# A four-layer graph network on one core: PSUM operands in layer 3, edges loaded first, layer 0's sums turned by transposes, node stages in halves

## The chip, the core and the metric

The kernel runs on one NeuronCore of a Trainium2 chip. The metric is the device time of one execution in microseconds (us), lower is better. The core has five engines that run at the same time, each with its own list of instructions: TensorE (PE, with its weight loads shown apart as PEld), VectorE (DVE), ScalarE (ACT), GpSimd (POOL) and SyncE (SP). DMA transfers are issued from the queues of SP, ACT and POOL. SBUF is the memory that all engines work on; PSUM is the one PE writes its products to, in banks of 512 float32 per partition.

## The reference

The input is a graph of 12,500 nodes with 32 features and 212,500 edges, sorted by destination (200,000 drawn ones and a loop for every node). Four layers follow one another, each as `x = layernorm(x + layer(x))`:

```python
# layer 0: weighted gather, segment sum, matmul
z = segment_sum(x[src] * edge_weight[:, None], dst) @ W
# layer 1: an MLP on edges with two batch norms, summed by source node
ef = concat([x[src], x[dst]])
h = relu(batch_norm(ef @ W1 + b1)); h = relu(batch_norm(h @ W2 + b2))
out = segment_sum(h, src)
# layer 2: two graph convolutions, norm = rsqrt(deg)[src] * rsqrt(deg)[dst]
h = h @ W; agg = segment_sum(h[src] * norm, dst) + h / deg + b
# layer 3: a 32x32 matrix per edge, six steps of a GRU
w_e = (relu(e_feat @ en1.T + b) @ en2.T + b).reshape(-1, 32, 32)
for _ in range(6):
    msg = einsum('ei,eio->eo', h[src], w_e)
    h = gru_cell(relu(segment_sum(msg, dst) + conv_bias), h)
```

## The kernel before

**Tiling.** Edges are padded to 128 x J with J = 1664 tile columns; a column is 128 edges, a chunk is CB = 32 columns, and NCH = 52 chunks are one pass over the edges. Nodes lie in SBUF as 128 partitions x NH = 98 columns x 32 features. A flag `crowded` (L658), worked out from the edges, selects between this path and a slower one that isn't executed here.

**Gathers and scatters.** A column of 128 rows is fetched by one indirect DMA that POOL issues (`gather`, L325, all recorded as L326). Scatters of 128 rows stand at L1686 (records of edges, by source, `rec_t`) and L1152 (`own_t`). A pass over the edges is 1664 of these on POOL.

**Stages in order.**
1. *Head*: SP loads the weights, then `by_tiles` (L582) loads dst, src and edge weights in rows of tiles, turns them with PE transposes (L606) and copies them out of PSUM on DVE (L607). The survey counts edges per node by one-hots on DVE (L377) and matmuls (L385). `places` (L396) makes the starts of nodes from the counts and tests that no tile of 128 edges begins too many nodes: it builds one-hots of each node's start (`oh_tile`, `oh_high`, L456), multiplies them on PE in 98 matmuls (L464) and takes the maximum (L466). The flag ends the head. Then the scatters by source node run.
2. *Layer 0's segment sum*: `slot_sum` (L984) reads the records chunk by chunk (`load`, L1721). A comparison of each edge's slot with an iota makes a mask; PE multiplies it with the edges' values into `acc` (L917); DVE keeps the block of its own (`part`, L927) and runs a scan over the columns (`running`, L934, with the comparison `on` at L938, the carry copy at L949, the scan at L952); ACT reorders (`by8`, L964); PE sums quarters back with `stack` (L1004, `back`), ACT copies to `o` and SP stores a table. At its end 98 gathers fetch the nodes' sums (`agg`).
3. *Node stage of layer 0*: transposes of `agg`, product with W, layernorm over all 98 columns, transposes of x, product with layer 1's weights, two tables written.
4. *Layer 1*: first pass with 26 gathers of runs (`run_rows`) and 1664 of `gq`, second pass without gathers, `slot_sum` again, 98 gathers, layernorm.
5. *Layer 2*: `kept` and `both` are made from x over all columns (L1145 to L1150), 98 scatters, and two convolutions of 1664 gathers each. Their comparisons use `iota_q`, a copy of iota in PSUM, and their `part` is in PSUM.
6. *Layer 3* (`layer3_tiles`, L1284): six steps. For each chunk DVE makes `near` (L1299, a comparison from SBUF into PSUM), ACT copies it to `mask`; 32 columns are gathered from the states in two halves; for each pair of columns DVE makes `prod` (L1322), PE multiplies with the edge's hidden values into `m` (L1330), ACT writes `outer` (L1337). Then PE makes `sums` (L917) and `acc` (L1354, L1362). The remaining work of a chunk (scan, by8, GRU gates, new state; L1367 to L1428) is spread over the pairs of the next chunk by the table `later`. Buffers: `g` 4, `eh` 3, `prod` and `m` 2, `near`, `sums`, `acc` and `gates` 1 (a PSUM bank each; `m` two banks a buffer).
7. *End*: a last layernorm per slot and 98 gathers of nodes.

**What sets the order.** The kernel is written in a tile framework: its scheduler places instructions on each engine's list, and dependencies between tiles follow from the regions that are read and written. A pool gives a tile so many buffers; a new tile of the same tag waits until the oldest buffer has been read.

Of the kernel before, what the change touches and what calls it, by code (L numbers as in the profile page):

```python
# [45 lines left out]
P = 128  # L46
# [28 lines left out]
MAGIC = 12582912.0  # L75

# [7 lines left out]
def tile_gnn(ctx: ExitStack, tc: tile.TileContext, a: dict, out: bass.AP):  # L84
# [6 lines left out]
    def sb(pool, shape, dt, name, **kw):  # L91
        return pool.tile(shape, dt, name=name, tag=name, **kw)

# [187 lines left out]
    def transposed(psum, xt, x):  # L281

        for g0 in range(0, CG, 4):
            n = min(4, CG - g0)
            t = sb(psum, [P, 4, P], F32, "tp")
            for k in range(n):
                g = g0 + k
                nc.tensor.transpose(t[:, k, :], x[:, 4 * g : 4 * g + 4, :].rearrange("p c f -> p (c f)"), ident)
            nc.vector.tensor_copy(xt[:, g0 : g0 + n, :], t[:, 0:n, :])

    def linear(psum, xt, w, width, use):

        for g in range(CG):
            t = sb(psum, [P, 4, width], F32, f"lin{width}")
            nc.tensor.matmul(
                t.rearrange("p c f -> p (c f)"), xt[:, g, :], w.rearrange("p c f -> p (c f)"), start=True, stop=True
            )
            use(g, t)
# [4 lines left out]
    def layernorm(name, x, d, y):  # L303

        with tc.tile_pool(name=f"ln_{name}", bufs=1) as work:
            s = sb(work, [P, NH, F], F32, "s")
            q = sb(work, [P, NH, F], F32, "q")
            m = sb(work, [P, NH], F32, "m")
            v = sb(work, [P, NH], F32, "v")
            nc.vector.tensor_add(s, x[:, 0:NH, :], d[:, 0:NH, :])  # L310
            nc.vector.tensor_reduce(out=m, in_=s, axis=AX, op=ALU.add)
            nc.vector.tensor_scalar(m, m, 1.0 / F, None, op0=ALU.mult)
            nc.vector.tensor_tensor(s, s, m.unsqueeze(2).to_broadcast([P, NH, F]), op=ALU.subtract)
# [4 lines left out]
            nc.vector.tensor_tensor(y[:, 0:NH, :], s, v.unsqueeze(2).to_broadcast([P, NH, F]), op=ALU.mult)  # L318

    def node_array(pool, name):  # L320
        t = sb(pool, [P, C, F], F32, name)
        nc.vector.memset(t[:, NH:C, :], 0.0)
        return t

# [23 lines left out]
    slots_ = ctx.enter_context(tc.tile_pool(name="slots", bufs=1))  # L348
# [47 lines left out]
    def places(work, psum, k, count, bad=None):  # L396
# [41 lines left out]
        if bad is not None:  # L438
# [5 lines left out]

            nc.vector.tensor_copy(at[:, 0, :], start[k])
            nc.vector.tensor_scalar(at[:, 1, :], at[:, 0, :], 7, None, op0=ALU.arith_shift_right)
            nc.vector.tensor_scalar(at[:, 2, :], at[:, 0, :], 14, None, op0=ALU.arith_shift_right)
            nc.vector.tensor_scalar(at[:, 1, :], at[:, 1, :], 127, None, op0=ALU.bitwise_and)
            nc.vector.tensor_copy(atf, at)
            nc.vector.scalar_tensor_tensor(atf[:, 2, :], atf[:, 2, :], 1.0, some, op0=ALU.add, op1=ALU.mult)  # L450
            nc.vector.tensor_scalar(atf[:, 2, :], atf[:, 2, :], -1.0, None, op0=ALU.add)
            tiles = J // P
            x = sb(work, [P, NH, P], BF, "oh_tile", bufs=1)
            y = sb(work, [P, NH, tiles], BF, "oh_high", bufs=1)
            for t, w_, d in ((x, P, atf[:, 1, :]), (y, tiles, atf[:, 2, :])):
                nc.vector.tensor_tensor(  # L456
                    t,
                    iota[:, 0:w_].unsqueeze(1).to_broadcast([P, NH, w_]),
                    d.unsqueeze(2).to_broadcast([P, NH, w_]),
                    op=ALU.is_equal,  # L460
                )
            starts = sb(psum, [P, tiles], F32, "starts")
            for h_ in range(NH):
                nc.tensor.matmul(starts, x[:, h_, :], y[:, h_, :], start=h_ == 0, stop=h_ == NH - 1)  # L464
            most = sb(work, [P, 1], F32, "most")
            nc.vector.tensor_reduce(out=most, in_=starts, axis=AX, op=ALU.max)  # L466
            nc.vector.tensor_scalar(most, most, WS - 0.5, None, op0=ALU.is_gt)
# [114 lines left out]
    def by_tiles(work, psum, name, to, firsts=None):  # L582

        v = a[name].rearrange("(b t p) -> t b p", p=P, t=P)
        whole = v.dtype == I32
        t = sb(work, [P, J // P, P], v.dtype, "by_i" if whole else "by_f")
        nc.sync.dma_start(t, v)
        if whole:
            f = sb(work, [P, J // P, P], F32, "by_f")
            nc.vector.tensor_copy(f, t)  # L590
            if name == "src":
# [5 lines left out]
                nc.sync.dma_start(saved["lo_row"].rearrange("o (b t p) -> t (o b) p", p=P, t=P), b)  # L597
# [4 lines left out]
        for b0 in range(0, J // P, 4):  # L602
# [4 lines left out]
            nc.vector.tensor_copy(to[:, b0 * P : (b0 + n) * P], u[:, 0:n, :].rearrange("p b t -> p (b t)"))  # L607
# [57 lines left out]
    fast_.close()  # L665

# [317 lines left out]
    def slot_sum(name, table, fill, agg, k="d", first=None):  # L984


        W, R8, slot_, going_, iota_w_ = (
            (W_D, R8_D, slot, going, iota_w) if k == "d" else (WS, P, slot_s, going_s, iota_s)
        )
        with tc.tile_pool(name=f"sl_{name}", bufs=2) as work, tc.tile_pool(  # L990
# [3 lines left out]
            for c in range(NCH):  # L994
# [7 lines left out]
                back = sb(psum, [R8, KB, F], F32, "back", bufs=1)  # L1002
                for b in range(KB):
                    nc.tensor.matmul(back[:, b, :], by8[:, b, :], stack, start=True, stop=True)  # L1004
                o = sb(work, [R8, KB, F], F32, "o")
                nc.scalar.activation(o, back, AF.Copy)
                nc.sync.dma_start(by_chunk(table, c, R8), o)
        for c in range(NH):
            gather(agg[:, c, :], table, slot_end[k][:, c : c + 1])
# [127 lines left out]
    def layer2_tiles(x):  # L1137

        spread = []
        with tc.tile_pool(name="n2", bufs=1) as n2:  # L1140
# [4 lines left out]
            nc.vector.tensor_tensor(both[:, :, 0:F], x[:, 0:NH, :], wide, op=ALU.mult)  # L1145
            nc.vector.tensor_copy(both[:, :, F], slot_end["d"])
            write_table("t2s", both, F + 1)
            kept = sb(n2, [P, NH, F + 1], F32, "kept")
            nc.scalar.activation(kept[:, :, 0:F], x[:, 0:NH, :], AF.Copy)
            nc.vector.tensor_copy(kept[:, :, F], root)  # L1150
            for c in range(NH):
# [54 lines left out]
        def fetch_a(work, c):  # L1206
            t = sb(work, [P, CB, F + 1], F32, "g33", bufs=3)
            for j in range(CB):
                gather(t[:, j, :], tables["t2s"], idx_d[:, c * CB + j : c * CB + j + 1])
# [31 lines left out]
        def fetch_b(work, c):  # L1241
            g = sb(work, [P, CB, F], F32, "g", bufs=3)
            for j in range(CB):
                gather(g[:, j, :], sums[0], idx_t[:, c * CB + j : c * CB + j + 1])
# [39 lines left out]
    def layer3_tiles():  # L1284

        def step(k, old_, new, mhs):
            with tc.tile_pool(name=f"l3{k}", bufs=2) as work, tc.tile_pool(
# [4 lines left out]

                def at(p):
# [3 lines left out]
                for c in range(NCH):  # L1297
                    near = sb(psum, [P, CB, W], F32, "near")
# [3 lines left out]
                        iota_w.unsqueeze(1).to_broadcast([P, CB, W]),  # L1302
# [8 lines left out]
                    for b in range(2):  # L1311
                        t0 = c * CB + b * HB
                        g = sb(work, [P, HB, F], F32, "g", bufs=4)
                        for j in range(HB):
                            gather(g[:, j, :], old_, idx_t[:, t0 + j : t0 + j + 1])
# [28 lines left out]
                    sums_ = sb(psum, [P, CB, W], F32, "sums")  # L1344
# [22 lines left out]
                    def run_on(c=c, acc=acc, v={}):  # L1367
# [6 lines left out]
                            iota_w,  # L1374
                            lambda out: nc.scalar.activation(out, acc.rearrange("p (t w) -> p w t", w=W), AF.Copy),  # L1375
                        )
# [36 lines left out]
                    def first_two(st=st):  # L1413
                        rz = st["rz"] = sb(work, [R8, KB, 2, F], F32, "rz")
                        nc.scalar.activation(rz, st["gates"][:, :, 0:2, :], AF.Sigmoid)
                        n = st["n"] = sb(work, [R8, KB, F], F32, "n")
# [3 lines left out]
                    def third(st=st):  # L1420
                        nc.scalar.activation(st["n"], st["n"], AF.Tanh)

                    def stored(st=st, old=old, c=c):
                        d = sb(work, [R8, KB, F], F32, "d")
                        nc.vector.tensor_sub(d, old, st["n"])
                        nc.vector.tensor_mul(d, d, st["rz"][:, :, 1, :])
                        nc.vector.tensor_add(d, st["n"], d)
# [131 lines left out]
    def by_source_tiles():  # L1559
# [143 lines left out]
        slot_all = sb(src, [P, J + 1], F32, "slot_s")  # L1703
# [5 lines left out]
        with tc.tile_pool(name="n0t", bufs=1) as n0:  # L1709
            ends = [sb(n0, [P, P], F32, f"row{p}") for p in (0, P - 1)]  # L1710
# [8 lines left out]
            with tc.tile_pool(name="l0t", bufs=3) as rec, tc.tile_pool(name="l0p", bufs=2, space=PSUM) as pp:  # L1719

                def load(c):  # L1721
# [8 lines left out]
                    nc.vector.tensor_copy(idx_s[:, js], t[:, :, F])  # L1730
# [8 lines left out]
                    nc.vector.tensor_copy(es, e)  # L1739
# [15 lines left out]
                slot_sum("l0", sums_s[0], fill, agg, "s", lambda c: loaded.update({c: load(c)}))  # L1755
            aggt = sb(n0, [P, CG, P], F32, "aggt")
            z = sb(n0, [P, C, F], F32, "z")
            with tc.tile_pool(name="p0t", bufs=2, space=PSUM) as psum:
                transposed(psum, aggt, agg)
                linear(psum, aggt, w0, F, lambda g, t: nc.vector.tensor_copy(z[:, 4 * g : 4 * g + 4, :], t))  # L1760
            layernorm("0t", x, z, x)

        with tc.tile_pool(name="n1t", bufs=1) as n1:
            pt, qt = sb(n1, [P, C, F], F32, "pt"), sb(n1, [P, C, F], F32, "qt")
            xt = sb(n1, [P, CG, P], F32, "xt")
            with tc.tile_pool(name="p1t", bufs=2, space=PSUM) as psum:
                transposed(psum, xt, x)

                def use(g, t):
                    nc.scalar.activation(pt[:, 4 * g : 4 * g + 4, :], t[:, :, 0:F], AF.Copy)  # L1770
                    nc.vector.tensor_tensor(qt[:, 4 * g : 4 * g + 4, :], t[:, :, F:], bias(b1_row, 4), op=ALU.add)

                linear(psum, xt, w1, 2 * F, use)
            write_table("t1q", qt)
            nc.sync.dma_start(tables["t1p"].rearrange("(c p) f -> p c f", p=P)[:, 0:NH, :], pt[:, 0:NH, :])
# [44 lines left out]
        with ExitStack() as l1:  # L1820
# [4 lines left out]
            with tc.tile_pool(name="p1at", bufs=2, space=PSUM) as psum, tc.tile_pool(  # L1825
# [10 lines left out]
                def fetch(c):  # L1836
                    gq = gqs[c] = sb(wide, [P, CB, F], F32, "gq", bufs=3)
                    for j in range(CB):
                        gather(gq[:, j, :], tables["t1q"], idx_s[:, c * CB + j : c * CB + j + 1])
# [83 lines left out]
            with tc.tile_pool(name="p1dt", bufs=2, space=PSUM) as pd:  # L1923
# [16 lines left out]
                slot_sum("l1", sums_s[1], fill, agg, "s")  # L1940
# [223 lines left out]
```

## Time and profile before

| | us |
|---|---|
| median of 3 runs (lowest to highest) | 23281.31 (23269.91 to 23287.24) |
| profiled execution | 23284.4 |
| its span in the profile | 23282.1 |
| granted TensorE clock, mean | 0.791 |
| busy: PE / DVE / ACT / POOL | 15635.5 / 10162.4 / 7142.4 / 16401.7 |

The profile is of one execution. It gives busy time by engine, the span in 40 slices, the chain of work that ended last, and groups of instructions: line, engine, operation, `out<-in`, shapes, count, then busy us and mean ns of one, then the idle time ahead of them and what ended it. Further views of the trace list an engine's waits (`line <- releaser: us in total, times, longest us`), a timeline of single instructions (start us, us, engine, line, operation, idle time ahead), and busy time by engine in chosen stretches of the span. Line numbers are those of the code above. POOL's part in a gather or scatter is the issue of it; the transfer follows on DMA engines.

### The profile page before, as it was taken

The page shows a single profiled execution, that of the slowest core. Times are in us where ns is not written, and L with a number is a line of the kernel's source. Part 1 is how long each engine was busy: PE and PEld are TensorE (multiplying, and loading weights), DVE is VectorE, ACT ScalarE, POOL GpSimd, SP SyncE. Part 2 cuts the span into 40 slices and gives each one's busy share as a digit, 9 for nine tenths or more (in the row PEclk, how much of TensorE's full clock was granted, in tenths as well). Part 3 has the DMA queues.
Part 4 walks back from the last instruction along what each step waited for, and adds up shares of the span by engine and source line. Part 5 has one row for each costly group of instructions (what it writes and reads, how often), then busy time and mean ns, then how long its engine had stood idle before and what let it go on. Part 6 is the DMA issues. An engine that isn't in the chain of part 4 may idle for free. (4 is left out here: it accounts for less than half of the span.)

```text
span 23282.1 us, 220871 instructions
## 1 busy us (share of the span) xinstructions
PE 15635.5 (67%) x73549; PEld 8950.4 (38%) x73549; DVE 10162.4 (44%) x16060; ACT 7142.4 (31%) x11020; POOL 16401.7 (70%) x17092
## 2 busy tenths in 40 slices
PE   4777644447122211148888888888888888888885
PEld 3666633335011111124444444444444444444442
DVE  7666434446111111124544444444444444544443
ACT  0333211114000000024444444444444444444442
POOL 2777357772777777777777777777777777777776
PEclk7555557778555555569999999999999999999997
DMA  2111223333111111112222222222222222222222
GB/s 66 43 42 41 58 78 94 94 94 116 17 17 16 16 19 19 19 42 69 67 69 65 68 69 64 68 67 69 64 69 69 67 64 69 67 66 67 68 69 57
DMA packets 1162538, 1372.56 MB, mean 59 GB/s; under 512 B 632424, under 2 KB 1024104, under 8 KB 1061320
## 3 DMA queue, kind: packets, MB, share of 16 engines
q1 hardware_dynamic: 597256, 952.79, 12.9%
q0 software_dynamic: 549184, 296.38, 8.2%
q10 hardware_dynamic: 14976, 109.06, 1.1%
q8 instruction: 627, 10.27, 0.2%
q14 instruction: 495, 4.06, 0.1%
HBM read 1130.72 MB, written 226.28 MB: 58 GB/s over the span
## 5 line engine op out<-in xcount | busy, mean ns | idle before, releaser
L326 POOL DMA_INDIRECT g<-states,idx_t x9984 | 9628.0, 964 | 3208.7 <-issue 2828.0
L1330 PE MATMUL m<-prod,eh 128*128 128x416 f32 x19968 | 8081.6, 548 | 1430.3 <-DVE prod L1322 1308.9
L1322 DVE TENSOR_TENSOR prod<-g,near 128x832 f32<-128x832 f32 x4992 | 5040.8, 1020 | 5142.6 <-DMA g<-states,idx_t 3243.4
L1330 PEld LDWEIGHTS m<-prod,eh 128*128 128x128 f32 x19968 | 3723.2, 199 | 5461.2 <-issue 4142.8
L1337 ACT ACTIVATE outer<-m 128x832 f32<-128x832 f32 x4992 | 4477.1, 897 | 4368.5 <-PE m L1330 4360.8
L917 PE MATMUL acc<-mask,g 128*128 128x52 f32 x1664 | 456.2, 420 | 3407.6 <-ACT g L1212 1725.8
L1686 POOL DMA_INDIRECT rec_t<-record,to x1664 | 1601.5, 962 | 675.0 <-issue 501.4
L326 POOL DMA_INDIRECT g<-sums,idx_t x1664 | 1571.6, 944 | 526.7 <-issue 492.2
L326 POOL DMA_INDIRECT gq<-t1q,idx_s x1664 | 1585.1, 953 | 507.1 <-issue 487.3
L326 POOL DMA_INDIRECT g<-t2s,idx_d x1664 | 1570.2, 944 | 515.2 <-issue 494.9
L1354 PE MATMUL acc<-outer,en_i 128*32 128x416 f32 x19968 | 1812.8, 515 | 0.0
L917 PEld LDWEIGHTS acc<-mask,g 128*128 128x128 f32 x1664 | 389.7, 321 | 3482.0 <-issue 1737.8
L1354 PEld LDWEIGHTS acc<-outer,en_i 128*32 128x32 f32 x19968 | 617.6, 110 | 979.7 <-issue 961.8
L1663 PE MATMUL place<-cur,xt 128*128 128x98 f32 x3326 | 990.7, 426 | 0.8 <-DVE own L1668 0.2
L952 DVE TENSOR_TENSOR_SCAN s<-on,part 128x429 f32<-128x429 f32 (+1 forms) x520 | 574.7, 1105 | 779.6 <-ACT part L1375 772.4
L964 ACT ACTIVATE by<-s 128x416 f32<-128x416 f32 (+1 forms) x520 | 293.9, 565 | 2013.8 <-DVE s L952 2013.8
L1663 PEld LDWEIGHTS place<-cur,xt 128*128 128x128 f32 x3326 | 814.9, 302 | 226.3 <-DVE own L1668 126.8
L927 DVE TENSOR_TENSOR part<-acc,blk 128x512 f32<-128x512 f32 (+1 forms) x208 | 134.3, 646 | 1663.0 <-PE acc L917 1663.0
L1375 ACT ACTIVATE part<-acc 128x416 f32<-128x416 f32 x312 | 162.1, 520 | 2261.8 <-PE acc L1362 2261.8
L1877 PE MATMUL t<-ident,gq 128*128 128x128 f32 x832 | 239.1, 383 | 899.6 <-DMA gq<-t1q,idx_s 830.7
L1662 ACT ACTIVATE cur<-next 128x98 f32<-128x98 f32 x1663 | 421.3, 253 | 1347.7 <-PE place L1663 790.0
L326 POOL DMA_INDIRECT agg<-sums_s,slot_end_s x196 | 185.0, 944 | 913.1 <-issue 912.2
(384 smaller groups left out, 16628.4 us busy)
## 6 DMA issues: line engine op xcount, KB each, us to landing
eh<-edge_h SPq DMA_DIRECT2D x624, 1024.0 KB
g<-states,idx_t POOLq DMA_INDIRECT x9984
edge_h<-eh ACTq DMA_DIRECT2D x104, 1024.0 KB
lows<-lo_row SPq DMA_DIRECT2D x52, 1024.0 KB
ht<-h_t SPq DMA_DIRECT2D x104, 512.0 KB
rt<-rec_t SPq DMA_DIRECT2D x52, 544.0 KB
rec_t<-record,to POOLq DMA_INDIRECT x1664
attr<-in_edge_attr SPq DMA_DIRECT2D x52, 512.0 KB
```

What stands on the lines that cost most here:

```text
L326: nc.gpsimd.indirect_dma_start(out=to, out_offset=None, in_=table, in_offset=bass.IndirectOffsetOnAxis(ap=idx, axis=0))
L917: nc.tensor.matmul(acc[:, 4 * g : 4 * g + 4, :].rearrange("p t w -> p (t w)"), v, mask[:, 4 * g : 4 * g + 4, :].rearrange("p t w -> p (t w)"),
L952: nc.vector.tensor_tensor_scan(s.rearrange("p w t -> p (w t)"), on.rearrange("p w t -> p (w t)"), part_.rearrange("p w t -> p (w t)"), ini ...
L964: nc.scalar.activation(by8.rearrange("p b (w t) -> p w b t", t=8), s[:, :, 1:].rearrange("p w (b t) -> p w b t", t=8), AF.Copy)
L1322: nc.vector.tensor_tensor(prod, g[:, j : j + 2, :].unsqueeze(3).to_broadcast([P, 2, F, W]), near[:, jj : jj + 2, :].unsqueeze(2).to_broadc ...
L1330: nc.tensor.matmul(m[:, i, 0 : F * W], eh[:, j + i, :], prod[:, i].rearrange("p f w -> p (f w)"), start=True, stop=True,)
L1337: nc.scalar.activation(outer[:, :, jj : jj + 2, :].rearrange("k f t w -> k t f w"), m[:, :, 0 : F * W].rearrange("k t (f w) -> k t f w", w=W),
L1354: nc.tensor.matmul(acc[q * F : (q + 1) * F, :], en2_i[:, i, :], outer[:, i].rearrange("k t w -> k (t w)"), start=i < 4, stop=i >= F - 3, s ...
L1662: nc.scalar.activation(cur, nxt, AF.Copy)
L1663: nc.tensor.matmul(place[:, j, :], xt[:, j, :], now, start=True, stop=False)
L1686: i = nc.gpsimd.indirect_dma_start(out=rec_t, out_offset=bass.IndirectOffsetOnAxis(ap=to[:, j : j + 1], axis=0), in_=t[:, j, :], in_offset ...
L1877: nc.tensor.matmul(t[:, g, :], gq[:, jj : jj + 4, :].rearrange("p j f -> p (j f)"), ident, start=True, stop=False)
```

## The change

- **Loads.** `src`, `dst` and `edge_weight` are the first loads on SP's queue, into tiles of their own. `by_tiles` uses them, writes `lo_row` from ACT's queue instead of SP's, and copies transposes out of PSUM on ACT instead of DVE.
- **Test of tiles.** In `places` the one-hots and 98 matmuls are replaced by two matmuls that fetch, for each node, the start of the node WS places on, and a comparison of the tile numbers of both.
- **Layer 0's segment sum.** Where `slot_sum` has a `first` (layer 0), `back` is made by four transposes of `by8` and a reduction on DVE. The copies to `idx_s` and `es` are on ACT; slots and the `ends` matrices are bf16 (slots in layer 1's masks too).
- **Halves.** `transposed`, `linear` and `layernorm` take a range of columns; layer 0's node stage and layer 1's layernorm, with the copies `kept` and `both`, are written for columns 0 to 51 and 52 to 97 in turn.
- **Gathers.** `gather_tiles` leaves out the columns beyond the last real edge (TILES = 1661) and sets their rows to zero.
- **Layer 3.** `near` and a copy of iota share one PSUM bank made once a step; `near` and `on` compare with that copy. `part` lies in the bank of `sums`. `n` after tanh, and the difference `old - n`, are written into the `gates` bank.

```diff
+TILES = -(-E // P)
+    for name in ("src", "dst", "edge_weight"):
+        raw[name] = sb(raw_pool, [P, J // P, P], a[name].dtype, f"raw_{name}")
+        nc.sync.dma_start(raw[name], a[name].rearrange("(b t p) -> t b p", p=P, t=P))
...
+    HALVES = ((0, -(-CG // 2)), (-(-CG // 2), CG))
...
+    def gather_tiles(to, table, idx, t0):
+
+        n = min(to.shape[1], max(0, TILES - t0))
+        if n < to.shape[1]:
+            nc.vector.memset(to[:, n:, :], 0.0)
+        for j in range(n):
+            gather(to[:, j, :], table, idx[:, t0 + j : t0 + j + 1])
...
+            far = sb(work, [P, 2, P], F32, "far")
+            for i in range(2):
+                nc.vector.tensor_scalar(far[:, i], iota, float(WS - 1 - i * P), part[:, 0:1], op0=ALU.add, op1=ALU.is_equal)
+            nc.tensor.matmul(below, far[:, 0], start[k], start=True, stop=False)
+            nc.tensor.matmul(below[:, 0 : NH - 1], far[:, 1], start[k][:, 1:NH], start=False, stop=True)
...
-                nc.sync.dma_start(saved["lo_row"].rearrange("o (b t p) -> t (o b) p", p=P, t=P), b)
+                nc.scalar.dma_start(saved["lo_row"].rearrange("o (b t p) -> t (o b) p", p=P, t=P), b)
...
-            nc.vector.tensor_copy(to[:, b0 * P : (b0 + n) * P], u[:, 0:n, :].rearrange("p b t -> p (b t)"))
+            nc.scalar.activation(to[:, b0 * P : (b0 + n) * P], u[:, 0:n, :].rearrange("p b t -> p (b t)"), AF.Copy)
...
+                if first is not None:
+                    back = sb(psum, [R8, KB, P], F32, "back", bufs=1)
+                    for b in range(KB):
+                        nc.tensor.transpose(back[:, b, :], by8[:, b, :], ident)
+                    nc.vector.tensor_reduce(
+                        out=o, in_=back.rearrange("r b (q f) -> r b f q", f=F), axis=AX, op=ALU.add
+                    )
...
+            for half in HALVES:
+                cs = slice(4 * half[0], min(NH, 4 * half[1]))
+                nc.scalar.activation(kept[:, cs, 0:F], x[:, cs, :], AF.Copy)
+                nc.vector.tensor_tensor(both[:, cs, 0:F], x[:, cs, :], wide[:, cs, :], op=ALU.mult)
+                nc.sync.dma_start(tables["t2s"].rearrange("(p c) f -> p c f", p=P)[:, cs, :], both[:, cs, :])
...
+                bank = sb(psum, [P, 512], F32, "near")
+                near = bank[:, 0:CW].rearrange("p (t w) -> p t w", w=W)
+                iota_q = bank[:, CW : CW + W]
+                nc.vector.tensor_copy(iota_q, iota_w)
...
-                        iota_w.unsqueeze(1).to_broadcast([P, CB, W]),
+                        iota_q.unsqueeze(1).to_broadcast([P, CB, W]),
...
-                    sums_ = sb(psum, [P, CB, W], F32, "sums")
+                    sums_ = sb(psum, [P, 512], F32, "sums")[:, 0:CW].rearrange("p (t w) -> p t w", w=W)
...
-                            iota_w,
+                            iota_q,
                             lambda out: nc.scalar.activation(out, acc.rearrange("p (t w) -> p w t", w=W), AF.Copy),
+                            sb(psum, [P, 512], F32, "sums")[:, 0 : W * (CB + 1)].rearrange("p (w t) -> p w t", w=W),
...
-                            nc.scalar.activation(st["n"], st["n"], AF.Tanh)
+                        nc.scalar.activation(st["gates"][:, :, 0, :], st["n"], AF.Tanh)
...
-                        nc.vector.tensor_sub(d, old, st["n"])
-                        nc.vector.tensor_mul(d, d, st["rz"][:, :, 1, :])
-                        nc.vector.tensor_add(d, st["n"], d)
+                        n, e = st["gates"][:, :, 0, :], st["gates"][:, :, 1, :]
+                        nc.vector.tensor_sub(e, old, n)
+                        nc.vector.tensor_mul(d, e, st["rz"][:, :, 1, :])
+                        nc.vector.tensor_add(d, n, d)
...
-        slot_all = sb(src, [P, J + 1], F32, "slot_s")
+        slot_all = sb(src, [P, J + 1], BF, "slot_s")
-            ends = [sb(n0, [P, P], F32, f"row{p}") for p in (0, P - 1)]
+            ends = [sb(n0, [P, P], BF, f"row{p}") for p in (0, P - 1)]
-                    nc.vector.tensor_copy(idx_s[:, js], t[:, :, F])
+                    nc.scalar.activation(idx_s[:, js], t[:, :, F], AF.Copy)
-                    nc.vector.tensor_copy(es, e)
+                    nc.scalar.activation(es, e, AF.Copy)
...
+                for h, half in enumerate(HALVES):
+                    transposed(psum, aggt, agg, half)
+                    linear(
+                        psum, aggt, w0, F, lambda g, t: nc.vector.tensor_copy(z[:, 4 * g : 4 * g + 4, :], t), half
+                    )
+                    layernorm(f"0t{h}", x, z, x, half)
+                    transposed(psum, aggt, x, half)
+                    linear(psum, aggt, w1, 2 * F, use, half)
...
-            layernorm("1t", x, agg, x)
+            for h, half in enumerate(HALVES):
+                layernorm(f"1t{h}", x, agg, x, half)
```

## The prediction

> **What bounds the kernel now.** I began with the page's busy times: POOL 70%, PE 67%, nothing else above 44%. The slices of the span show POOL at 7 tenths nearly everywhere with PE at 8 to 9 in the second half, so both are candidates. The chain that ended last is led by POOL's gathers of 128 rows, and the groups say how these run:
>
> ```profile
> L326 POOL DMA_INDIRECT g<-states,idx_t x9984 | 9628.0, 964 | 3208.7 <-issue 2828.0
> L326 POOL DMA_INDIRECT g<-sums,idx_t x1664 | 1571.6, 944 | 526.7 <-issue 492.2
> L326 POOL DMA_INDIRECT gq<-t1q,idx_s x1664 | 1585.1, 953 | 507.1 <-issue 487.3
> ```
>
> Behind each gather stand about 0.305 us put down to issue, in which POOL waits for nobody. A gather costs 1.249 us in layer 2 (0.944 + 0.305) and 1.269 in layer 3 (0.964 + 0.305). So in the streams of gathers POOL is full, although it reads 70%, and the time is streams plus the gaps between them. The wait list of POOL gives the gaps:
>
> ```profile
> POOL rec_t L1686 <- PE place L1663: 167.8, 1, 167.8
> ...
> POOL agg L326 <- issue: 912.2, 193, 431.2
> ...
> POOL run_rows L326 <- DVE eh L1814: 67.2, 1, 67.2
> ...
> POOL own_t L1152 <- ACT kept L1149: 28.1, 1, 28.1
> ```
>
> Reading along the span: POOL starts its stream of scatters at 477.6 us; 1664 scatters run to 2586; 431.2 us go to layer 0's segment sum; 98 gathers; 67.2; layer 1's gathers to 5334; a second pass of 423 us; 98 gathers, 28.1, 98 scatters; two streams of layer 2 (6039 to 10214); six streams of layer 3 (10231 to 23051) with gaps of 26 to 35 us; 232 us of end. The six streams are 12,820 of 23,282 us. There the work by engine is:
>
> ```profile
> 10231.00:23050.00 12819.00, 11281.29 (x51060) 5560.58 (x51060) 6302.42 (x8103) 5472.72 (x7174) 9627.19 (x9984) 0.96 0.24 67
> ```
>
> Columns are PE, PEld, DVE, ACT, POOL. Over 312 chunks (6 steps of 52) PE is busy 36.2 us a chunk, and POOL needs 32 x 1.269 = 40.6 us. **PE has 4.4 us to spare in a chunk**, and POOL sets the pace.
>
> **Layer 3's operands in PSUM.** Why are its gathers 20 ns longer than layer 2's? Most are not: they take 0.94, and two in every chunk are long. The timeline of POOL around one chunk:
>
> ```profile
> 16224.94 1.21 POOL L326 DMA_INDIRECT g<-states,idx_t  x1 [0.30 <-issue]
> 16226.45 0.94 POOL L326 DMA_INDIRECT g<-states,idx_t  x1 [0.30 <-issue]
> ...
> 16236.44 1.37 POOL L326 DMA_INDIRECT g<-states,idx_t  x1 [0.30 <-issue]
> 16238.12 0.94 POOL L326 DMA_INDIRECT g<-states,idx_t  x1 [0.30 <-issue]
> ```
>
> and DVE's of the same moments:
>
> ```profile
> 16224.74 0.60 DVE L1299 TENSOR_TENSOR near<-slot,iota_w 128x416 f32<-128x416 bf16 x1
> ...
> 16236.31 0.18 DVE L949 COPY part<-s 128x13 f32<-128x13 f32 x1
> 16236.40 0.60 DVE L938 TENSOR_TENSOR on<-going,iota_w 128x429 f32<-128x429 bf16 x1
> ```
>
> Over 14,600 to 16,600 us the long gathers fall together with these operations: all 49 near cost 253 ns beyond 944, all 49 on (with the copy ahead of it) 427 ns; together 34 us in 1576 gathers. The operations at L1425 and L1426, also of two SBUF tiles, cost gathers nothing. In layer 2 the same two comparisons take iota from PSUM and the copy goes into PSUM:
>
> ```profile
> L938 DVE TENSOR_TENSOR on<-going,iota_q 128x429 f32<-128x429 bf16 x49 | 29.0, 593 | 0.0
> L976 DVE TENSOR_TENSOR mask<-slot,iota_q 128x416 f32<-128x416 bf16 x48 | 27.9, 581 | 0.0
> ```
>
> and there gathers average 944. The change makes layer 3 like layer 2. It takes away (253 + 427) ns x 312 chunks = **212 us**, bounds 0 (the cause is something else in layer 3) and 225 (34.25 us of excess in 1576 gathers is 0.0217 us, x 9984 = 217, and some at the edges). I take 212. DVE's own time does not grow: near and on take 600 ns from SBUF in layer 3, 593 and 581 with PSUM in layer 2; the scan 1079 and 1049.
>
> [...]
>
> The new cost: part now lies in the bank of sums (one buffer), and near and iota_q fill one bank for the whole step (one buffer, as before). PE's sums of a chunk must wait until the scan of the chunk before has read part. In the changed program's order the scan stands in the first quarter of a chunk on DVE and most of sums at the end on PE, so there are about 20 us between them. Cost 0; above, PE's whole reserve, 4.4 less the 0.7 that POOL gains = 3.7 us a chunk, hides it.
>
> **The head.** Before, SP first issues about a hundred weight loads and fills; the first edge load is issued at 81.5 us:
>
> ```profile
> 81.51 8.50 SPq L587 DMA_DIRECT2D by_i<-in_dst  x1
> 90.05 7.04 SPq L587 DMA_DIRECT2D by_i<-in_src  x1
> ```
>
> DVE begins on it at 103.5 and its first one-hot of the survey starts at 153.6. Issued first, the load is there at about 1 + 8.5 = 9.5 us. DVE did 10.4 us ahead of 103.5 and 49.3 up to 153.6; 12 evictions of 0.58 = 7.0 us leave it for ACT, idle here. Some 48 of the remaining 53 us come after 9.5. Two of DVE's small preparations of weights (en_i waited 20.3 us for its load, gru_s 13.6) stand inside this stretch, and their loads now queue behind the edges: I count 6 us. The first one-hot is then at 63.5: **-90** (bounds -35, if DVE sits behind these weights as long as it did, 20 + 14 + about 20 of shift, and -96). What follows (153.6 to 397) is bound by DVE's one-hots and stays. Then the test of tiles loses one-hots of 13.22 and 1.49 us and a wait of 2.9 for PE's 98 matmuls, and gets about six operations of 0.2 in place of nine: **-17** (-14 to -18). These are on the path: the first scatter needs the flag.
>
> **Layer 0's segment sum** (431.2 us, 52 chunks of 7.97; clock 0.50). No engine is full: of 410 us PE is busy 315, DVE 200, ACT 96. The loop is acc on PE, part and scan on DVE, by on ACT, back on PE:
>
> ```profile
> L917 PE MATMUL acc<-mask,v 128*128 128x64 f32 x816 | 186.4, 423 | 0.0
> L1004 PE MATMUL back<-stack,by 128*128 128x32 f32 x408 | 97.6, 403 | 93.7 <-ACT by L964 93.7
> ```
>
> A chunk has 6.15 us of PE's work and 1.8 of waiting for by. The change replaces 8 passes of back (1.9 us) by 4 transposes (4 x 0.24, as the transposes of L606: 1.0), and 4 f32 passes of ends by 2 in bf16 (-0.6). PE's order also changes: three chunks now share a cycle in which acc of the next chunk stands ahead of most transposes, so part of the 1.8 is filled. Against it, DVE gets a reduction of 128x512 from PSUM, by part's 692 ns 0.7 us, and gives es (225) to ACT: about 4.2 us a chunk, still under PE's 4.7. Bounds per chunk: 7.97 (the chain through DVE takes back all) and 5.85 (all saved and 0.6 of waiting filled): 0 to -110. Nearest is the saving of PE's work less a part that the chain keeps: 1.15 us x 52 = **-60**.
>
> **Halves.** In the timeline of the 67.2 us gap, DVE's LN takes 24 us (3144 to 3168), PE's transposes and products 23 (to 3191), and writing the tables with the wait for it 16 (to 3207). Columns 0 to 51 are gathered 57 us before the last column, so their part of that lies beside gathers. The second half keeps 46 of 98 columns of the first two (22) and about 12 of the last, with 4 for more small operations: 38, **-29** (-20 to -35). Layer 1's node stage: in 28.1 us the first scatter waits for all of kept; POOL's wait on kept<-root now ends in the middle of the first half: **-17** (-10 to -27). The columns of the second half run beside scatters.
>
> **Gathers left out.** 3 of 1664 in each of nine streams: 27 x 1.25 = 34 us; a step's drain after the last gather holds one more pair, so I take 3 for layer 1, 5 for layer 2 and 18 for layer 3: **-26** (-15 to -34).
>
> **One price against.** Slots become bf16 in the masks of layers 0 and 1; beside layer 1's gathers (953) such a comparison could cost up to on's 427 ns x 52 = 22 us, or take away part of the 9 ns above 944 (15 us). I take 0.
>
> **Sum:** -90 - 17 - 60 - 29 - 17 - 26 - 212 = -451. The profiled execution took 23,284.4 (span 23,282.1): 22,833; the median of the runs is 3 lower: **22,830**.
>
> **Rivals.** (1) The delay of gathers stays or moves to other operations of layer 3, as L1425 shows that two SBUF tiles alone are no cause: 22,830 + 212 = 23,042; 10%. For it: the copy and on can't be told apart in the trace. Against: layer 2. (2) The head and layer 0 give little (DVE waits for weights, the reduction lengthens the chain): 55 + 60 less: 22,945; 13%. (3) Slower: PE becomes the bound in layer 3, because sums wait for the scan in the shared bank. The other terms save 239 us, 0.77 us over 312 chunks; so it decides from a chunk of 40.6 + 0.8 = 41.4 us, that is 5.2 us more of waiting on PE. A wait of 8 us, in which a chunk's acc would wait for sums behind the scan, gives 36.2 + 8 = 44.2: 312 x 3.6 - 239 = +880, 24,160; 3%, as the written order leaves 20 us. (4) The head is not what is late: the scatters wait for other loads; inside (2). The forecast itself: 74%.
>
> **Range.** Best terms together -546, which won't all happen; 22,740 to 22,970 takes in (2) and leaves (1) and (3) out. Measurements of this kernel tell apart about 0.2% (47 us). Faster 0.96, same 0.01, slower 0.03.
>
> **What would show it.** Layer 3's gathers at 944 and steps of 2075 us instead of 2113; the first scatter at 370; the gap of 431 at about 371; 67 at 38; 28 at 11. Wrong if near or on still lengthen gathers, or PE's sums wait for the scan.

## The result and the profile after

The changed kernel takes 22,876.16 us (median of 4 runs, 22,873.81 to 22,876.86), the kernel before 23,278.42 (4 runs). The ratio is 0.9827, with a 95% interval of 0.981 to 0.9844: 402 us less, where 451 were forecast. Its profiled execution has a span of 22,872.0 us, 410.1 less than before. Here are the lines of POOL's wait list that answer to those shown of before (`line <- releaser: us in total, times, longest us`; in the first line the longest wait, 363.9, is layer 0's segment sum; the rest of it are the 0.3 us between gathers):

```profile
POOL agg L349 <- issue: 422.8, 194, 363.9
POOL rec_t L1709 <- PE place L1686: 153.2, 1, 153.2
...
POOL run_rows L349 <- DMA t1p<-pt: 37.9, 1, 37.9
...
POOL own_t L1171 <- DVE kept L1164: 11.2, 1, 11.2
```

The gaps of 431, 67 and 28 us have become 364, 38 and 11, close to the 371, 38 and 11 that were forecast. The page's groups of gathers, and the busy times (PE, PEld, DVE, ACT, POOL) over layer 3's six streams:

```profile
L349 POOL DMA_INDIRECT g<-states,idx_t x9966 | 9404.6, 944 | 3188.6 <-issue 2800.9
...
L349 POOL DMA_INDIRECT gq<-t1q,idx_s x1661 | 1583.2, 953 | 506.2 <-issue 485.1
L349 POOL DMA_INDIRECT g<-sums,idx_t x1661 | 1568.1, 944 | 525.5 <-issue 491.5
```

```profile
10066.00:22643.00 12577.00, 10968.68 (x51057) 5532.64 (x51058) 6316.44 (x8113) 5476.63 (x7172) 9404.27 (x9966) 0.96 0.25 68
```

Layer 3's gathers are at layer 2's 944 ns, 20 below before, and 9966 instead of 9984. PE is busy 35.2 us of the 40.3 a chunk now has, step gaps included, so POOL still sets the pace. Going along the span by the starts and ends of POOL's streams gives the account of the 410 us:

| stage | before | after | change | forecast |
|---|---|---|---|---|
| head, to the first scatter | 477.6 | 424.5 | -53.1 | -107 |
| scatters | 2108.7 | 2109.7 | +1.0 | 0 |
| layer 0's segment sum | 431.2 | 363.9 | -67.3 | -60 |
| 98 agg gathers, layer 0 and 1 | 244.1 | 252.7 | +8.6 | 0 |
| node stage of layer 0 | 67.2 | 37.9 | -29.3 | -29 |
| layer 1, both passes | 2549.7 | 2549.2 | -0.6 | -3 |
| layer 1's norm, own_t scatters | 151.7 | 137.0 | -14.7 | -17 |
| layer 2's two streams, with the waits ahead of, between and behind them | 4200.5 | 4191.4 | -9.1 | -5 |
| layer 3's six streams | 12670.5 | 12439.8 | -230.7 | -230 |
| gaps between steps | 149.3 | 137.3 | -12.0 | 0 |

The rest, the end of the kernel, is 3 us shorter. The forecast is missed in one place: the head gave half, 54 us less than its 107. The other rows together gave 13 us more than theirs.

Layer 3's -230.7 can be taken apart. The durations of its gathers beyond 944 ns add up to 203.1 us before and to -3.3 after, which is 206; the 18 gathers left out, at 1.25 us each, are 22.5; 2 remain.

### The profile page after: what moved, and what is told of

Read it like the earlier page. It is cut to its first block, busy times and chain, and to the rows that moved or that the text cites. A ratio compares the mean times of both kernels' runs of the same rounds, so it can differ in the third digit from the quotient of the medians.

```text
span 22872.0 us, 220938 instructions
## 1 busy us (share of the span) xinstructions
PE 15242.0 (67%) x73143; PEld 8842.0 (39%) x73143; DVE 10178.0 (44%) x16026; ACT 7156.1 (31%) x11087; POOL 16181.8 (71%) x17065
## 5 line engine op out<-in xcount | busy, mean ns | idle before, releaser
L349 POOL DMA_INDIRECT g<-states,idx_t x9966 | 9404.6, 944 | 3188.6 <-issue 2800.9
L1395 ACT ACTIVATE sums<-acc 128x416 f32<-128x416 f32 x312 | 156.6, 502 | 2185.4 <-PE acc L1382 2149.5
L928 PEld LDWEIGHTS sums<-mask,g 128*128 128x128 f32 x4992 | 656.0, 192 | 293.1 <-issue 280.3
```

Of the source, the lines that this page charges most:

```text
L349: nc.gpsimd.indirect_dma_start(out=to, out_offset=None, in_=table, in_offset=bass.IndirectOffsetOnAxis(ap=idx, axis=0))
L928: nc.tensor.matmul(acc[:, 4 * g : 4 * g + 4, :].rearrange("p t w -> p (t w)"), v, mask[:, 4 * g : 4 * g + 4, :].rearrange("p t w -> p (t w)"),
```

## The experiments

A few words on reading them. The intervals of the ratios are about 0.17% (40 us) to either side, while the four runs of a changed kernel on one chip lie within 9 us of each other (those of the kernel before within 23; on the two slow chips told of below the spread is larger); so an effect of 10 to 60 us is read from the stage it belongs to in the profile, with the time beside it.

**What holds the head.** The wait lists of DVE and ACT in the first 118 us of the changed kernel name it:

```profile
DVE slot_h L642 <- DMA t2s<-zero: 43.1, 1, 43.1
DVE gru_s L242 <- DMA gru_t<-in_L_gnn_gru_bhh: 12.3, 1, 12.3
```

```profile
ACT weight_d L617 <- DMA t2s<-zero: 58.9, 1, 58.9
```

A cast of edge data waits 43 us for the last fill of zeros, data it has nothing to do with. In the code the tile `zero` lies in a pool of its own that is closed after the fills are issued, and `slot_h` and `weight_d`, allocated later, wait for the last fill. Theory: they take its space. Rival: the head is limited by the weight loads or the rate of transfers. Two kernels take the wait away in two ways. The first lets `zero` live in the pool of the raw edge loads:

```diff
-        zero = sb(pool, [P, P - NH, 2 * F], F32, "zero")
+        zero = sb(raw_pool, [P, P - NH, 2 * F], F32, "zero")
```

> The changed kernel with the tile of zeros placed beside the raw edge loads, so that no tile of the survey takes over its space while the fills are still reading it. Theory: in the changed kernel DVE (43.1 us at the cast slot_h) and ACT wait for the last fill, because slot_h and weight_d lie where the zeros lay. Then that wait goes: first one-hot at about 72 us instead of 114.6, time 22,876 - 43 = 22,833. The tile twos now waits for a store on a DMA semaphore that the fills count on too; if that holds it, only 20 us are gained: 22,856. Rival (the head is limited by the weight loads or by the rate of transfers): no change, 22,876.

Measured: 22,816.39 us (22,815.41 to 22,821.02; ratio 0.9801, 0.9785 to 0.9817), 60 less than the changed kernel. The one-hots of the survey in the first 130 us of its profile (duration in ns, then first and last start in that stretch):

```profile
L399 DVE TENSOR_TENSOR oh<-twos,klo x19: 2284/2284/2287, 58.1 to 128.8; 128x4096 bf16<-128x4096 bf16 x19
```

The first starts at 58.1 us instead of 114.6, and the first scatter at 363.0 instead of 424.5. The gain is larger than expected because `gru_s`, whose wait of 12.3 us the expectation had left in, now stands behind the first one-hots in DVE's order (at 64.3 us), where it waits for nothing. Another 4.8 us come from the gap that ends in the first scatter. `twos`, which I feared might wait in its place, waits for nothing.

The second kernel writes the fills behind the survey:

```diff
-    with tc.tile_pool(name="zeros", bufs=1) as pool:
-        zero = sb(pool, [P, P - NH, 2 * F], F32, "zero")
...
     raw_.close()
+    with tc.tile_pool(name="zeros", bufs=1) as pool:
+        zero = sb(pool, [P, P - NH, 2 * F], F32, "zero")
...
```

> The changed kernel with the zeros and all fills issued after the survey's tiles instead of before them. Theory (the fills are what DVE waits for, and with them gone DVE's order also puts the addition gru_s behind the first one-hots): first one-hot at about 60 us, 43 + 12 us earlier, time 22,876 - 55 = 22,821. If the fills, now beside the one-hots and the gathers of run_rows, delay those: 10 us of it come back. Rival (weight loads limit the head): 22,876, the first one-hot stays at 115.

Measured: 22,818.17 us (ratio 0.9801, 0.9785 to 0.9818); the first one-hot at 60.2, the first scatter at 369.9. The theory holds by both ways. The rival falls: loads and fills are the same transfers in both, in the first kernel in the same order, and in the second the fills are still issued between 62 and 97 us, in the changed kernel between 57 and 83. What both change is that no tile of the survey takes over the space of `zero`.

**What layer 0's gain is made of.** I had put the larger part on the four transposes. This kernel goes back to matmuls with `stack`, all else as changed:

```diff
-                if first is not None:
+                if False:
                     back = sb(psum, [R8, KB, P], F32, "back", bufs=1)
```

> The changed kernel with layer 0's sums turned back by matmuls with stack and copied by ACT, as before; the bf16 ends and the copies on ACT stay. Theory: the transposes save about 0.9 us of PE's work a chunk and the rest of the gap's 67 us comes from ends, so 52 x 0.9 = 47 us come back: 22,923, gap between scatters and agg gathers 411 instead of 364. Rival (all of the gain is the cheaper ends and the moved copies): 22,876. Rival (the reduction on DVE costs as much as it saves): 22,870.

Measured: 22,865.02 us (ratio 0.9822, 0.9805 to 0.9838), 11 faster, not 47 slower. The gap and PE's wait in layer 0's sum, here with matmuls,

```profile
POOL agg L349 <- issue: 414.7, 195, 355.5
```

```profile
PE ends L1759 <- DVE slot_s L1757: 143.3, 25, 85.9
PE acc L928 <- ACT v L1772: 1.0, 1, 1.0
PE acc L928 <- DVE mask L987: 0.9, 2, 0.6
PE back L1022 <- ACT by L975: 0.3, 1, 0.3
```

and the same wait list of the changed kernel, with transposes:

```profile
PE ends L1759 <- DVE slot_s L1757: 120.8, 19, 85.3
PE back L1015 <- ACT by L975: 71.2, 47, 2.8
```

(85 us in the first line of both are PE's idle time before the stage.) With transposes PE is busy 239 of 350 us, with matmuls 278 of 340: PE works less and waits more. So the gain did not come from the transposes, and two more kernels undo the other edits one at a time, on top of this one. First the copies to `es` and `idx_s`, back on DVE:

```diff
-                    nc.scalar.activation(idx_s[:, js], t[:, :, F], AF.Copy)
+                    nc.vector.tensor_copy(idx_s[:, js], t[:, :, F])
-                    nc.scalar.activation(es, e, AF.Copy)
+                    nc.vector.tensor_copy(es, e)
```

> back_matmul with the copies to es and idx_s on DVE again; bf16 ends stay. Layer 0's gap in the profile is to tell what made its gain: 355 with copies on ACT. Theory (PE's shorter ends and its order make the gain; DVE has room: 187 of 340 us): 355 to 365. Rival (ACT's copies break the wait of ends for DVE): over 400, up to the 431 of before.

Then slots and `ends` back in float32:

```diff
-        slot_all = sb(src, [P, J + 1], BF, "slot_s")
+        slot_all = sb(src, [P, J + 1], F32, "slot_s")
-            ends = [sb(n0, [P, P], BF, f"row{p}") for p in (0, P - 1)]
+            ends = [sb(n0, [P, P], F32, f"row{p}") for p in (0, P - 1)]
```

> back_matmul with slots and the ends matrices in float32 again; copies to es and idx_s stay on ACT. Theory (two bf16 passes save 0.6 us of PE in a chunk): 52 x 0.6 = 31 us more, gap 386; layer 1's first pass unchanged to 5 us. Rival (the order of PE's work makes the gain alone): 355.

These two ran on a chip on which every kernel, the one before included (36,105.64 us), is half as long again. There PE, DVE and ACT stand still for stretches in which POOL issues gathers or scatters, and POOL then waits for them. In the kernel with both repairs (below) ACT works 88 of its 5,394 us in layer 3's streams while POOL issues (gathers and the 0.3 us between them); in the changed kernel's profile it is 5,442 of 5,477. Five us of the kernel with both repairs (its stretch, then busy time and instructions of PE, PEld, DVE, ACT and POOL):

```profile
20005.00:20010.00 5.00, 0.00 (x0) 0.00 (x0) 0.00 (x0) 0.00 (x0) 3.78 (x5) 0.50 0.10 13
```

Why the engines stand still there stays open. The times of the two kernels (35,875.88 and 35,864.43) are of no use here, and layer 1's first pass could not be judged. Layer 0's sum, which has no gathers, is not touched: back_matmul's code gives 355.5 us on its own chip and, with the head's repair, 355.4 on this one. The gaps are, first with the copies on DVE, then with float32 ends:

```profile
POOL agg L349 <- issue: 452.8, 195, 393.6
```

```profile
POOL agg L349 <- issue: 447.0, 195, 387.9
```

So the copies on ACT are worth 38.1 us and the bf16 ends 32.4 (31 expected); together 70.5 of the 75.7 by which 355.5 is under the 431.2 of before, if the two add up, which no run undoing both shows. The transposes cost 8.5. With the copies on DVE, PE's wait of `back` for `by` is there again, as it was before the change; here is this stage in the kernel with the copies on DVE, then in the kernel before:

```profile
PE back L1022 <- ACT by L975: 97.5, 50, 2.8
```

```profile
PE back L1004 <- ACT by L964: 96.5, 50, 2.8
```

I had expected a gap of 355 to 365 there, reading from DVE's 187 busy us of 340 that it has room. That was wrong: busy time is again 186 of 345 us, and the stage is 38 us longer. The reading that fits is that the copies stand in the chain from PE through DVE and back, which room elsewhere doesn't shorten. Why the transposes bring back 71 us of that wait was not tried; PE's order and DVE's queue, with 35 us of reductions more, both change with them.

**The halves.**

```diff
-    HALVES = ((0, -(-CG // 2)), (-(-CG // 2), CG))
+    HALVES = ((0, CG),)
```

> The changed kernel with HALVES set to one part of all columns. Theory: the node stages lose their cover, +29 us in layer 0's and +17 in layer 1's gap, and the gathers and scatters beside which the halves ran lose what they are delayed by (4.7 + 3.9 + 2.2 = 11 us): 22,876 + 46 - 11 = 22,911. Rival (the 11 us are not from the halves): 22,922.

Measured: 22,904.26 us (ratio 0.9838, 0.9822 to 0.9855), 28 slower. Its gaps, and its agg gathers of layer 0 against those of the changed kernel (mean ns behind the busy us):

```profile
POOL run_rows L349 <- DMA t1p<-pt: 63.2, 1, 63.2
...
POOL own_t L1171 <- ACT kept L1167: 28.3, 1, 28.3
```

```profile
L349 POOL DMA_INDIRECT agg<-sums_s,slot_end_s x98 | 92.5, 944 | 393.4 <-issue 393.1 <-DMA agg<-sums_s,slot_end_s 0.3
```

```profile
L349 POOL DMA_INDIRECT agg<-sums_s,slot_end_s x98 | 97.2, 992 | 393.5 <-issue 393.2 <-DMA agg<-sums_s,slot_end_s 0.3
```

The halves hide 25 and 17 us. The layernorm that now runs beside the gathers costs these 4.7 us here: four of its operations with two SBUF inputs (L325, L328, L329 and L333) each run into the start of one gather and make it 1.32, 1.58, 0.67 and 1.07 us longer. It costs 3.9 at layer 1's agg and, with the product `both` (L1168) beside it, 2.1 at the scatters: 11 us that the prediction had not counted, as expected of this run. Of the 29 us that layer 0's node stage lost in the table, 4 are not the halves' (67.2 before, 63.2 here); what made them was not tried.

**Layer 3's gathers.** The prediction left open why L1425, with two SBUF tiles, costs gathers nothing. The traces show that it is a matter of phase, that is, of how the start of a gather falls against the DVE operation. In layer 3 of the kernel before, where near or on began 38 ns or more before the gather and still ran 0.13 us after the gather's start, the gather was longer than 0.944 us by (end of the DVE operation - start of the gather - 0.13 us). The lines in the prediction show it: near ends at 16225.34, 0.40 us after the start of its gather, which takes 0.27 more than 0.94; on ends at 16237.00, 0.56 after, and its gather takes 0.43 more.

Over the whole layer this holds to 0.01 us for the 288 gathers that on lengthens (122 us in all) and the 295 that near lengthens (77 us); two more near, which begin 2 and 3 ns ahead of their gathers, leave these at 0.94 us. Over 14,600 to 16,600 us L1425 nearly always begins 680 ns or more after a gather's start and costs 0; the five times in the whole layer that it runs into a gather's start, it ends 135 to 229 ns after it and costs 8 to 103. In layer 2's second stream an addition (L1252) that ends 131 to 233 ns after a gather's start costs 1 to 106. For the scan (L952), which reads two SBUF tiles too, the gather is 0.06 us shorter than by this sum (17 gathers, 6 us in all). So layer 3's near and on sat in a bad phase and L1425 in a good one. Four kernels put operands back into SBUF: all three, near alone, on alone, part alone (the last is the one that tells the copy of the carry apart from on).

```diff
-                        iota_q.unsqueeze(1).to_broadcast([P, CB, W]),
+                        iota_w.unsqueeze(1).to_broadcast([P, CB, W]),
```

```diff
                             going,
-                            iota_q,
+                            iota_w,
```

```diff
-                            sb(psum, [P, 512], F32, "sums")[:, 0 : W * (CB + 1)].rearrange("p (w t) -> p w t", w=W),
```

> The changed kernel with layer 3's near and on compared with iota in SBUF and part in SBUF, as before the change. Theory: a gather needs SBUF about 0.13 us after its start; a DVE operation of two SBUF tiles that is running then holds it until that operation's end. near and on come back into that position: layer 3's mean gather 964 instead of 944 ns, 312 x 0.68 = 212 us: 23,088. Rival (the gain came from other edits of layer 3, such as n and d in PSUM): 22,876.

> The changed kernel with near alone compared with iota in SBUF. Theory: 312 x 0.253 = 79 us: 22,955, each delayed gather longer by (end of near - start of the gather - 0.13 us). Rival (on or the copy caused all of it): 22,876.

> The changed kernel with on alone compared with iota in SBUF; part stays in PSUM. Theory: 312 x 0.427 = 133 us: 23,009. Rival (the copy of the carry from SBUF to SBUF was the cause, on only came behind it): 22,876.

> The changed kernel with part alone in SBUF, so that the carry is copied from SBUF to SBUF and the scan reads two SBUF tiles. Theory: the copy has one SBUF input and ends 0.05 us after the gather's start, the scan starts with it, so neither is in the way: 22,876 (to +10). Rival (the copy was the cause): 22,876 + 133 = 23,009. The scan takes 1079 ns instead of 1049 where it waits for the gather's own access.

They ran on a chip where the kernel before takes 23,245.11 us and the changed one was not run, so I compare the six streams. These are 12,439.8 us in the changed kernel's profile, and 12,439.6 and 12,439.5 in those of back_matmul and zero_raw, which leave layer 3 as it is:

| kernel | time | six streams | more than changed | expected |
|---|---|---|---|---|
| all three in SBUF (4 runs) | 23,131.27 | 12,698.4 | 259 | 212 |
| near (1 run) | 22,936.39 | 12,506.5 | 67 | 79 |
| on (1 run) | 22,940.95 | 12,519.1 | 79 | 133 |
| part (1 run) | 22,939.67 | 12,511.3 | 72 | 0 |

All three give the gain back (ratio to before 0.9951, 0.9934 to 0.9967), so the gain is these operands and not `n` or `d`. But they don't give it back by the same parts: of the delay of gathers in this kernel, near makes 67 us, on only 0.7, and the scan 190. A chunk of it, DVE then POOL:

```profile
14565.70 1.05 DVE L963 TENSOR_TENSOR_SCAN s<-on,part 128x429 f32<-128x429 f32 x1 [2.60 <-ACT part L1395]
```

```profile
14565.92 1.59 POOL L349 DMA_INDIRECT g<-states,idx_t  x1 [0.30 <-issue]
```

The scan begins 0.2 us ahead of a gather here and holds it 0.64 us; in the kernel before it cost 6 us in all, and on 122. That the sum is near the expected 212 is therefore partly luck: the expectation had near and on in it and no scan.

near alone comes out (67 us in 297 gathers). on is a cause by itself, against the rival that it was the copy; only its place has moved. It now holds 270 gathers, ending 276 to 559 ns after their start, for 296 ns on the mean and not 424. And part alone costs 72 where I expected nothing. The timelines of that kernel show why; DVE and POOL at one chunk,

```profile
12338.94 1.05 DVE L963 TENSOR_TENSOR_SCAN s<-on,part 128x429 f32<-128x429 f32 x1 [2.05 <-ACT part L1395]
```

```profile
12339.03 1.71 POOL L349 DMA_INDIRECT g<-states,idx_t  x1 [0.30 <-DMA g<-states,idx_t]
```

and at the next:

```profile
12379.72 1.10 DVE L963 TENSOR_TENSOR_SCAN s<-on,part 128x429 f32<-128x429 f32 x1 [2.02 <-ACT part L1395]
```

```profile
12379.74 0.95 POOL L349 DMA_INDIRECT g<-states,idx_t  x1 [0.30 <-DMA g<-states,idx_t]
```

In the first the scan begins 90 ns ahead of the gather, which then takes 1.71 us instead of 0.94. In the second it begins 16 ns ahead, and the gather is not delayed but the scan is: 1.10 us instead of 1.05. In this kernel the 92 scans that begin 44 ns or more ahead hold a gather, nearly all for 704 to 818 ns, 71 us in all; those that begin later don't hold it, and the ones up to 44 ns ahead wait themselves. In the kernel before 289 of 306 scans stood on the harmless side, -12 to +19 ns from the gather's start. The expectation reckoned with the delay that the traces show, but took the phase of before for granted. The 44 ns are not a limit for every operation: in the kernel before on held gathers from 38 ns ahead.

So in these runs a comparison that begins 38 ns or more ahead of a gather, or a scan that begins 44 ns or more ahead, makes the gather longer as told above, to 0.01 us for the comparisons of the kernel before and 0.06 us short of that for the scan. A scan that begins later, close to the gather's start, waits itself, by at most 75 ns (1128 against 1053) and not for the gather's 944.

**The two repairs together**: `zero` in the raw pool, and `back` by matmuls.

> zero_raw and back_matmul together. Theory (both are local to their stages): 402 + 60 + 11 = 473 us below the kernel before, on the chip of the first four runs 22,805; the gap of layer 0's segment sum 355 as in back_matmul, the first scatter at 363 as in zero_raw. Rival (one gives back what the other gains): not under 22,816.

> zero_raw and back_matmul together once more, on another chip, since on the chip of the last three runs the gathers of every kernel, the one before included, held the other engines up. Theory: the head and layer 0's sum are independent, 402 + 60 + 11 = 473 us below the kernel before (ratio 0.9797; on the chip of the first four runs 22,805). Rival: they overlap, not below 0.980.

Both ran on chips of the kind told of above, where engines stand still beside gathers: 35,789.47 us against 36,105.64 before (ratio 0.9913, 0.9897 to 0.993), and 35,777.68 against 36,095.74 (0.9911, 0.9894 to 0.9927). The parts keep their size: first scatter at 363.3 and 368.4 us, layer 0's sum 355.4 and 355.3. The changed kernel was not run on these chips, so neither the sum nor the rival is settled by their times. The time of the two together on a chip like the first is left open; 22,805 remains a sum.

## Why the prediction was right, and where it was not

- **Bound and layer 3 right.** "Layer 3's gathers at 944" and "steps of 2075 us instead of 2113" came as 944 and 2073, for -231 where 212 + 18 were forecast (206 + 22.5 by the traces). Rival (1) fell: no operation of layer 3 makes a gather of the changed kernel longer by more than 18 ns (the longest takes 962). What I gave as evidence against two SBUF inputs as the cause, L1425 at nothing, was a matter of phase. PE did not become the bound, and in PE's wait list of the six streams sums never waits for the scan: rival (3) fell. DVE's near and on with one operand in PSUM take 596 ns, 600 and 599 before, so the operand in PSUM made them no longer:

```profile
L949 DVE TENSOR_TENSOR on<-going,near 128x429 f32<-128x429 bf16 x50 | 29.8, 596 | 0.0
L1320 DVE TENSOR_TENSOR near<-slot,near 128x416 f32<-128x416 bf16 x50 | 29.8, 596 | 1.7
```

- **Head wrong in size**: "The first one-hot is then at 63.5: -90" was 114.6, -39. The step that failed is the count of what stands in the way: I counted the two weights, "I count 6 us", and they took 12.3 (all of it gru_s), and I missed a wait of 43.1 on the fills, which stands in front of slot_h in the changed program's order. With the wait gone the one-hot starts at 58.1, and the head is 114.6 us shorter than before, near the 107 forecast. Rival (2) named a late DVE for the weights; it was late for the fills.
- **Test of tiles right**: -17 forecast. From the copy of the counts (`count`) to the flag DVE takes 10.1 us instead of 26.6, 16.5 less. The gap that ends in the first scatter fell by 14.6 (167.8 to 153.2); it lies between 146 and 153 us in the other kernels with this code, and no kernel undid this edit alone.
- **Layer 0 right in size by wrong parts**: "replaces 8 passes of back" was to bring most of -60. It was -67, made of -38 by the copies that I gave no price as a gain, -32 by ends (-31 forecast) and +8.5 by the transposes; 5 more are not accounted for. That the size fits is luck: the step that carried most of it had the wrong sign.
- **Halves right** in both gaps (25 and 17 us by the run without them, 29 and 17 forecast); the gathers and scatters beside them got 11 us longer, which I had not priced although the rows of near and on gave the price.
- **Gathers left out right.** Layer 2's two streams lost 8.3 us, as 6 x 1.25 = 7.5 and some, where 5 were forecast; layer 3's 18 gathers are 22.5 of its 231, where 18 were. The slots in bf16 cost layer 1's gathers nothing (953 before and after).
- **Not forecast**: the gaps between steps are 12 us shorter, mostly at the second and fourth. With near, on and part back in SBUF they are as short (137.4 against 137.3), so it is none of these; no run was made to find the cause.

## What to carry to other kernels

A transfer that is moved to the front is worth only as much as the consumers' own waits allow: before pricing it, list for each early consumer what its *tile* waits for, including the readers of whatever lay in that space before. When POOL issues gathers back to back, look for DVE operations with two SBUF inputs that are running when a gather starts; one operand in PSUM took them out here, and a few hundred nanoseconds a chunk were 206 us over this kernel. An operation that costs nothing today may only be in a harmless phase: the scan cost 6 us in one kernel and 190 in another. A gain that comes out in the right size should still be taken apart, since one of its parts may be a loss.

## What was not expected of the hardware

- In the kernel before, near and on that began 38 ns or more ahead of a gather made it longer by their own end minus the gather's start minus 0.13 us, to 0.01 us in 583 gathers; the scan did by 0.06 us less. The subtraction L328 of the changed kernel's layernorm did so for 1.58 us. Additions of two SBUF tiles (L1252, L1427) that ended less than 0.13 us after a gather's start left it at 0.94 us.
- The outcome of the scan against the gather turned on a few nanoseconds: at 44 ns ahead one scan waited some 75 ns, and another held its gather for about 815.
- One and the same kernel, the one before, took 23,245 and 23,280 us on two chips and 36,106 and 36,096 on two others, where engines stood still beside gathers.
